# Attention and non-local block: one subtraction of the maxima a block, the weighted sum kept in the result's tile, and the halves of one sum of exponentials added ahead of the ones

## The chip, the cores and the metric

The kernel runs on one core of one Trainium2 chip. The metric is the device time of one execution in microseconds (us), as the median of several runs. TensorE (PE in the profile) does the matmuls, VectorE (DVE), ScalarE (ACT) and GpSimd (POOL) the rest of the arithmetic; SyncE (SP) issues DMAs, and GpSimd issues the DMAs that add while they copy.

## The reference

The input x has 2 images of 256 channels and 64 x 64 = 4096 places. Two layers follow each other. Only the first, an attention with 8 heads of 32 channels, is touched by most of the change:

```python
qkv = jnp.einsum('oc,bchw->bohw', w_qkv, x)
q, k, v = jnp.split(qkv, 3, axis=1)            # each to (b, 8, 32, 4096)
scores = jnp.einsum('bhdi,bhdj->bhij', q, k) / jnp.sqrt(32)
attn = jax.nn.softmax(scores, axis=-1)
out = jnp.einsum('bhij,bhdj->bhdi', attn, v)
x = jnp.einsum('oc,bchw->bohw', w_proj, out) + x
```

The second layer is a non-local block: two 1 x 1 convolutions and a third, two of them pooled 2 x 2, a softmax over 1024 pooled places, a weighted sum, a last convolution, a batch normalisation and the addition of x.

## The kernel before, in words

**Blocks and steps.** Four heads make a quad, so there are 2 images x 2 quads, numbered n = 0 to 3. The 4096 queries of a quad are cut into 8 blocks of 512 (i), so the attention has 32 blocks. A block goes over its 4096 keys in 32 steps of 128 (j). In a step (lines 534 to 569), for each of two pairs of heads, TensorE makes scores of 128 keys x 512 queries for two heads (`score`, L415) and ScalarE takes their exponential (L551). Then TensorE makes the weighted sum of the values of the step before for all four heads (`weigh`, L439), and VectorE adds it to the block's sum `num` (L450). In step 0 ScalarE copies instead of adding (L448).

**Scores by differences.** A pair of heads keeps one PSUM tile over several steps. At every fourth step (j % 4 == 0) the tile is begun anew: `subtract` (L427) writes minus the maximum of each query, as a product of ones with three bf16 terms of the maximum, and the scores of 128 keys are added to it. In the three steps after it, not the next keys are multiplied but the difference between the next keys and those before, so that the tile then holds the next scores. The keys of a quad (`k[n]`) lie in 8 chunks of 512, and four steps take the same 128 columns of four neighbouring chunks: chunk 1 - 0 lies in `kd[n]`, 2 - 1 in `mid_kd`, 3 - 2 in `kd[n]`, and for the upper four chunks in `last_kd`, `mid_kd`, `last_kd`. GpSimd makes these differences: L219 and L241 in the prologue, and at each change of quad L234 (twice 1024 columns) and L241.

**Maxima.** `maxima` finds the maximum of every query, a little over one block ahead of the exponentials: further products (L264), of which VectorE reduces plain ones (L276), while for half of heads 2 and 3's chunks ScalarE takes the positive part of a product with a difference (L283) and VectorE reduces the sum (L290). Each `advance(maxes)` issues two such products. They use `k`, `kd` and `last_kd`, but in block 0 of a later quad not `last_kd`. `negate` then makes the three terms on GpSimd (L141 to L145), and `make_rows` turns them with TensorE (L150).

**Sums of the exponentials.** A step has two tiles of exponentials: a single one of heads 0 and 1 (six buffers) and half of a double one of heads 2 and 3 (five buffers). `add` collects them: GpSimd adds the singles to the block's first single (L469) except that of step 31, which stays apart; the doubles are added by DMAs that add (L477), in turn to two partial sums. `normalize`, for the block before, is a generator that the steps of the next block advance at j = 2 and from j = 6 on (AFTER). At j = 2 it merges the two partial sums by one more such DMA (L483). At j = 6 TensorE multiplies what is left with ones (L495): for heads 0 and 1 the sum and step 31's exponentials, for heads 2 and 3 the two halves of the merged double, two rounds over four heads. ScalarE copies the denominators (L503), SyncE brings them into a form in which VectorE inverts few elements (L512 to L521), and some 18 steps later GpSimd multiplies `num` by them and writes the result's tile `y` (L526). The blocks that end a batch don't merge and have four rounds.

**What sets the order.** Each engine works off its own queue in order. The framework forms the queues from the program's order and the tiles' dependencies and adds the waits; `tc.issue_after(x)` puts an instruction behind x on x's engine. Beside the attention, `make` projects one piece of q, k or v of what comes next after steps 11, 19 and 27 (L186, L198).

**Second layer.** `non_local` keeps its running sums of exponentials in the tile `sum1`, of the same two buffers as `num` (L706).

Of the kernel before, what the change touches and what calls it, by code (L numbers as in the profile page):

```python
# [9 lines left out]
F32 = mybir.dt.float32  # L10
# [6 lines left out]
N = HH * WW  # L17
# [5 lines left out]
P = 128  # L23
# [12 lines left out]
def conv_attention(  # L36
# [131 lines left out]
    def make(what, n, i):  # L168
        b, qd = QUAD[n]
        if (b, i) not in held:  # L170
            name = f"x_{what}_{n}_{i}"
            if attending:
                held.clear()
                to = xs.tile([P, NC, NB], F32, tag="x", name=name)
            else:
                to = single(name)
            held[b, i] = load_x(b, i, to)
        xc = held[b, i]
        name = f"{what}_{b}_{qd}_{i}"
        pq = scratch(name)  # L180
        if what == "v":
            if i == 0:
                v[n] = qkv.tile([P, NJ, QH, D], F32, tag="v", name=f"v_{n}")
            for j in range(NB // P):
                for c in range(NC):
                    nc.tensor.matmul(  # L186
                        pq[:, bass.ts(j, P)],
                        xc[:, c, bass.ts(j, P)],
                        wv_sb[:, c, bass.ts(qd, P)],
                        start=(c == 0),  # L190
                        stop=(c == NC - 1),
                    )
                if j % 2 == 1:
                    yield
            nc.scalar.copy(v[n][:, bass.ts(i, NB // P)].rearrange("p j h d -> p (j h d)"), pq)
            return
        for c in range(NC):
            nc.tensor.matmul(  # L198
                pq,
                wqk_sb[:, c, qd, 0 if what == "q" else 1, :],  # L200
                xc[:, c, :],
                start=(c == 0),
                stop=(c == NC - 1),
            )
            yield
        if what == "q":
            to = q[n, i] = qkv.tile([P, NB], F32, tag="q", name=f"q_{n}_{i}", bufs=3)
        else:
            if i == 0:
                k[n] = qkv.tile([P, N], F32, tag="k", name=f"k_{n}")  # L210
            to = k[n][:, bass.ts(i, NB)]
        nc.scalar.copy(to, pq)
        if what == "k" and i % 4 == 2 and n == 0:
            between(n, i // 4)
        if what == "k" and i % 2 == 1 and n == 0:
            if i == 1:
                kd[n] = qkv.tile([P, NI // 4, NB], F32, tag="kd", name=f"kd_{n}")
            two = k[n][:, bass.ts(i // 2, 2 * NB)]
            nc.gpsimd.tensor_sub(  # L219
                (kd[n] if i < NI // 2 else last_kd)[:, i // 2 % (NI // 4), :],  # L220
                two[:, NB:],
                two[:, :NB],
            )
        elif what == "k" and i == NI // 2 - 1:
            kd[n] = qkv.tile([P, NI // 4, NB], F32, tag="kd", name=f"kd_{n}")
            differences(n, 0, kd[n])

    last_kd = const.tile([P, NI // 4, NB], F32, name="last_kd")  # L230

    def differences(n, half, to):
        two = k[n][:, bass.ts(half, N // 2)].rearrange("p (c t n) -> p c t n", t=2, n=NB)
        nc.gpsimd.tensor_sub(to, two[:, :, 1, :], two[:, :, 0, :])  # L234


    mid_kd = const.tile([P, 2, NB], F32, name="mid_kd")

    def between(n, half):
        two = k[n][:, N // 2 * half + NB :]  # L240
        nc.gpsimd.tensor_sub(mid_kd[:, half, :], two[:, NB : 2 * NB], two[:, :NB])  # L241

# [143 lines left out]
    def attend(b, y):  # L388
        class Block:


            def __init__(self, qd, i):
                self.n, self.qd, self.i = QUAD.index((b, qd)), qd, i
                self.name = f"{b}_{qd}_{i}"
                self.rows = self.n * NI + i
                self.num = None
                self.sums = {}
                self.last = []

        def keys(j):  # L400

            return j // 16 * 16 + j % 4 * 4 + j % 16 // 4

        def score(s, pair, blk, j):

            half, c, cols = j // 16, j % 4, bass.ts(j % 16 // 4, P)
            if c == 0:
                kj = k[blk.n][:, bass.ts(keys(j), P)]
            elif c == 2:
                kj = mid_kd[:, half, cols]  # L410
            else:
                kj = (last_kd if half else kd[blk.n])[:, c // 2, cols]
            for t in range(2):
                h = 2 * pair + t
                nc.tensor.matmul(  # L415
                    s[:, t, :],
                    kj[bass.ts(h, D), :],
                    q[blk.n, blk.i][bass.ts(h, D), :],
                    start=False,
                    stop=True,  # L420
                    skip_group_check=j % 4 > 0,
                )

        def subtract(s, pair, blk):
# [10 lines left out]
        def weigh(blk, j, p):  # L435

            w = scratch(f"w_{blk.name}_{j}")
            for h in range(QH):
                nc.tensor.matmul(  # L439
                    w[bass.ts(h, D), :],  # L440
                    v[blk.n][:, keys(j), h, :],
                    p[h // 2][:, h % 2, :],
                    start=True,
                    stop=True,
                )
            if j == 0:
                blk.num = work.tile([P, NB], F32, tag="num", name=f"num_{blk.name}")
                nc.scalar.copy(blk.num, w)  # L448
            else:
                nc.vector.tensor_add(blk.num, blk.num, w)  # L450

        DIRECT = 1
        added = None

        def add(blk, j, p, two):
            nonlocal added
            if j == 0:  # L460
                blk.sums[0] = p[0]
            elif j % 2 and (blk.n, blk.i) == (len(QUAD) - 1, NI - 1):

                if j == 1:
                    blk.last.append(p[0])
                else:
                    nc.vector.tensor_add(blk.last[0], blk.last[0], p[0])
            elif j < NJ - DIRECT:
                added = nc.gpsimd.tensor_add(blk.sums[0], blk.sums[0], p[0])  # L469
            else:  # L470
                blk.last.append(p[0])
            if j % 2:
                n = 1 + j // 2 % 2
                if j < 4:
                    blk.sums[n] = two
                else:
                    nc.gpsimd.dma_start(out=blk.sums[n], in_=two, accum_op=ALU.add)  # L477

        def normalize(blk):
            whole = [1, 2]  # L480
            if (blk.qd, blk.i) != (QUADS - 1, NI - 1):
                with tc.issue_after(added.ins):
                    nc.gpsimd.dma_start(out=blk.sums[1], in_=blk.sums[2], accum_op=ALU.add)  # L483
                whole = [1]
                yield
            den = scratch(f"den_{blk.name}")
            mine = [
                [blk.sums[0], *blk.last],
                [blk.sums[n][:, j] for j in range(2) for n in whole],
            ]  # L490
            for n in range(max(map(len, mine))):
                for h in range(QH):
                    those = mine[h // 2]
# [29 lines left out]
                for _ in range(13):  # L523
                    yield
            with tc.issue_after(added.ins):
                nc.gpsimd.tensor_mul(y[:, blk.qd, bass.ts(blk.i, NB)], blk.num, r)  # L526

        waiting, normal = None, iter(())
        for qd in range(QUADS):
            for i in range(NI):  # L530
# [3 lines left out]
                for j in range(NJ):  # L534
# [1 line left out]
                        two = double(f"p_{blk.name}_{j}_1")  # L536
                    p = [single(f"p_{blk.name}_{j}_0"), two[:, j % 2]]
                    for pair in (1, 0):
                        if j % 4 == 0:
                            s = both[pair] = scores(f"s_{blk.name}_{j}_{pair}")  # L540
                            subtract(s, pair, blk)
                            advance(maxes)
# [12 lines left out]
                            normal = normalize(waiting[0])  # L555
                    add(blk, j, p, two)
                    waiting = blk, j, p
                    if j == 2 or j >= AFTER:
                        advance(normal)
                    if j % 2 == 0:  # L560
                        make_rows()
                        if (i, j) == (0, 2) and blk.n > 0:
                            between(blk.n, 1)
                        if (i, j) == (0, NJ // 4) and blk.n > 0:
                            differences(blk.n, 1, last_kd)
                        if (i, j) == (NI - 1, NJ // 2 + 2) and blk.n + 1 < len(QUAD):
                            between(blk.n + 1, 0)
                    elif j % 8 == 3 and j > 8 and items:
                        advance(make(*items.pop(0)), 9)
        weigh(*waiting)  # L570
# [26 lines left out]

    def non_local(b, y, theta_w, phi_w):
        theta = [double(f"theta_{b}_{t}") for t in range(2)]
        theta = [t[:, a, c, :] for t in theta for a in range(2) for c in range(2)]  # L600

        kv = qkv.tile([P, M + NC * M + M - 2 * P], F32, tag="k", name=f"kv_{b}")
# [100 lines left out]
        def weigh(i, t, p):  # L703
            if t == 0:
                acc[i] = [scratch(f"y_{b}_{i}_0"), scratch(f"y_{b}_{i}_1")]
                acc[i].append(work.tile([P, NB], F32, tag="num", name=f"sum1_{b}_{i}"))  # L706
                nc.gpsimd.tensor_add(acc[i][NC], p[:, 0, :], p[:, 1, :])
            else:

# [65 lines left out]


    LEAD = 4
    AFTER = 6
    attending = False


# [77 lines left out]
```

## Time and profile before

| What | Value |
| --- | --- |
| Median of 3 runs | 3987.23 us (3986.58 to 3989.69) |
| Profiled execution, its own time | 3986.4 us |
| Its span, first to last instruction | 3984.6 us |
| Busy of the span: PE, DVE, POOL, ACT | 99%, 74%, 73%, 67% |
| Mean share of the DMA engines in an attention block | 0.80 (1253 to 1357 us) |
| An attention block with maxima | about 104 us |
| Granted clock of TensorE | 0.997 |

A line of the groups has the line of code, engine, operation, output and inputs, their shapes and the count, then the busy time in us and the mean of one in ns, then the idle time of the engine just before, and what ended it. A line of the timeline has the start and the duration in us; neighbours of one kind are merged (x8 is eight instructions), and brackets hold the idle time before. PE stands for matmuls, PEld for loads of weights. An f32 matmul appears as two instructions. Shapes such as 32*128 are rows x columns of the array that a matmul uses.

### The profile page before, as it was taken

To read this page: it belongs to the slowest core of one execution; us is meant where nothing else is said; L and a number is where in the kernel's file an instruction comes from. 1 tells how busy PE (TensorE), PEld (TensorE's weight loads), DVE (VectorE), ACT (ScalarE), POOL (GpSimd) and SP (SyncE) were. 2 spreads that over 40 slices of the span, in tenths; PEclk is the share of its full clock that TensorE was granted. 3 is DMA by queue.
4 is the path that set the end of the run, shared out by engine and by line. 5 is a ranking of instruction groups with operands and counts; after the bars stand their busy time and mean duration, and the time that the engine had idled before them with its cause. 6 is when DMAs were issued, how large, how long until landed. Compare 5 with 4: busy or idle time off the path is not lost.

```text
span 3984.6 us, 72269 instructions
## 1 busy us (share of the span) xinstructions
PE 3949.7 (99%) x28592; PEld 1450.9 (36%) x28592; DVE 2937.8 (74%) x5451; ACT 2671.5 (67%) x3328; POOL 2903.6 (73%) x1851
## 2 busy tenths in 40 slices
PE   8999999999999999999999999999999999999998
PEld 4333333333333333333333333333333333333333
DVE  5877877788777787774457877787888888884434
ACT  4777777777777777751137777777677777777121
POOL 1888888888888888871448888888888888886043
PEclk9999999999999999999999999999999999999999
DMA  1777877887777777880017788878787778778200
GB/s 56 146 160 165 166 165 164 170 166 163 165 162 164 163 165 164 170 198 8 22 39 163 165 166 166 173 165 170 162 173 164 164 165 166 163 163 182 66 16 27
DMA packets 113941, 569.56 MB, mean 143 GB/s; under 512 B 20296, under 2 KB 22600, under 8 KB 52416
## 3 DMA queue, kind: packets, MB, share of 16 engines
q0 software_dynamic: 68832, 501.25, 62.8%
q1 hardware_dynamic: 44080, 62.88, 4.5%
q8 instruction: 224, 3.67, 0.4%
q14 instruction: 117, 0.96, 0.1%
q10 hardware_dynamic: 688, 0.79, 0.1%
HBM read 54.78 MB, written 8.88 MB: 16 GB/s over the span
## 4 chain that ended last, share of the span: by engine, by line
PE 97%; DVE 2%; DMA 0%; ACT 0%; POOL 0%; issue 0%; DVEq 0%; ACTq 0%
PE w L439 26%; PE ps L264 26%; PE s L415 24%; PE y L715 6%; PE s L427 3%; PE q L198 2%; PE v L186 2%; PE k L198 2%; PE den L495 1%; PE g L640 1%; DVE r L729 1%; PE f L683 1%; PE proj L584 1%; PE f L749 1%; PE tp L624 0%; PE tp L620 0%
## 5 line engine op out<-in xcount | busy, mean ns | idle before, releaser
L469 POOL TENSOR_TENSOR p<-p,p 128x1024 f32<-128x1024 f32 x945 | 2324.7, 2460 | 557.0 <-ACT p L551 550.1
L551 ACT ACTIVATE p<-s 128x1024 f32<-128x1024 f32 x2048 | 2089.9, 1025 | 624.1 <-PE ps L264 408.5
L264 PE MATMUL ps<-k,q 32*128 32x512 f32 x6232 | 2049.0, 627 | 4.0 <-DVE part L276 1.7
L276 DVE TENSOR_REDUCE part<-ps 128x1 f32<-128x512 f32 x2136 | 1369.9, 686 | 574.2 <-PE ps L264 557.7
L439 PE MATMUL w<-p,v 128*32 128x512 f32 x8192 | 1091.0, 605 | 0.7 <-ACT p L551 0.7
L450 DVE TENSOR_TENSOR num<-num,w 128x512 f32<-128x512 f32 x992 | 681.4, 687 | 92.7 <-PE w L439 91.3
L290 DVE CUSTOM_DVE_ANT_0 ps<-ps,over 128x512 f32<-128x512 f32 x980 | 676.0, 693 | 32.1 <-PE ps L264 27.9
L264 PEld LDWEIGHTS ps<-k,q 32*128 32x128 f32 x6232 | 636.5, 183 | 55.7 <-DVE num L450 8.7
L283 ACT ACTIVATE over<-ps 128x512 f32<-128x512 f32 x916 | 543.2, 593 | 15.2 <-PE ps L264 14.0
L264 PE MATMUL ps<-kd,q 32*128 32x512 f32 x1056 | 518.2, 595 | 0.7 <-POOL kd L219 0.7
L415 PE MATMUL s<-q,k 32*128 32x512 f32 x2048 | 513.2, 590 | 0.0
L415 PE MATMUL s<-q,kd 32*128 32x512 f32 x2048 | 511.1, 616 | 0.4 <-ACT p L551 0.3
L415 PE MATMUL s<-q,mid_kd 32*128 32x512 f32 x2048 | 510.1, 614 | 0.0
L415 PE MATMUL s<-q,last_kd 32*128 32x512 f32 x2048 | 506.8, 614 | 0.0
L439 PEld LDWEIGHTS w<-p,v 128*32 128x32 f32 x8192 | 161.1, 108 | 799.0 <-DVE part L276 769.4
L264 PE MATMUL ps<-last_kd,q 32*128 32x512 f32 x904 | 437.4, 590 | 1.5 <-POOL last_kd L219 1.5
L477 POOL DMA_DIRECT2D p<-p x448 | 395.5, 883 | 33.4 <-ACT p L551 28.7
L415 PEld LDWEIGHTS s<-q,mid_kd 32*128 32x128 f32 x2048 | 173.0, 183 | 309.7 <-ACT over L283 197.1
L415 PEld LDWEIGHTS s<-q,kd 32*128 32x128 f32 x2048 | 174.6, 184 | 282.2 <-ACT over L283 177.8
L415 PEld LDWEIGHTS s<-q,last_kd 32*128 32x128 f32 x2048 | 173.1, 183 | 269.6 <-ACT over L283 164.3
L715 PE MATMUL y<-p,kv 128*128 128x512 f32 x512 | 240.0, 608 | 6.4 <-DVE r L729 6.4
L764 ACT ACTIVATE p<-f 128x1024 f32<-128x1024 f32 x64 | 65.6, 1025 | 248.4 <-PE f L749 219.1
(108 smaller groups left out, 2720.4 us busy)
## 6 DMA issues: line engine op xcount, KB each, us to landing
p<-p POOLq DMA_DIRECT2D x478, 1024.0 KB, 7.5
x_k<-in_x_dram SPq DMA_DIRECT2D x32, 512.0 KB
x_q<-in_x_dram SPq DMA_DIRECT2D x30, 512.0 KB
x_res<-in_x_dram SPq DMA_DIRECT2D x16, 512.0 KB
out_dram<-z SPq DMA_DIRECT2D x16, 512.0 KB
r<-flat SPq DMA_DIRECT2D x120, 64.0 KB
x_v<-in_x_dram SPq DMA_DIRECT2D x6, 512.0 KB
wqk_sb<-in_wqk_dram ACTq DMA_DIRECT2D x1, 512.0 KB
```

Of the source, the lines that this page charges most:

```text
L198: nc.tensor.matmul(pq, wqk_sb[:, c, qd, 0 if what == "q" else 1, :], xc[:, c, :], start=(c == 0), stop=(c == NC - 1),)
L264: nc.tensor.matmul(ps, q[n, i][bass.ts(h, D), bass.ts(g, P)], keys[bass.ts(h, D), :], start=True, stop=True,)
L276: reduced = nc.vector.tensor_reduce(part[:, g, h, j : j + 1], ps, AX.X, ALU.max)
L283: cut = nc.scalar.activation(over, ps, AF.Relu)
L290: reduced = nc.vector.tensor_tensor_reduce(out=ps, in0=ps, in1=over, scale=1.0, scalar=LEAST, op0=ALU.add, op1=ALU.max, accum_out=part[:, ...
L415: nc.tensor.matmul(s[:, t, :], kj[bass.ts(h, D), :], q[blk.n, blk.i][bass.ts(h, D), :], start=False, stop=True, skip_group_check=j % 4 > 0,)
L439: nc.tensor.matmul(w[bass.ts(h, D), :], v[blk.n][:, keys(j), h, :], p[h // 2][:, h % 2, :], start=True, stop=True,)
L450: nc.vector.tensor_add(blk.num, blk.num, w)
L469: added = nc.gpsimd.tensor_add(blk.sums[0], blk.sums[0], p[0])
L477: nc.gpsimd.dma_start(out=blk.sums[n], in_=two, accum_op=ALU.add)
L551: nc.scalar.activation(p[pair], s, AF.Exp, scale=scale)
L715: nc.tensor.matmul(acc[i][o], wg[:, 2 * t + j, bass.ts(o, P)], p[:, j, :], **edge)
```

## The change

1. Only step 0 of a block begins its two PSUM tiles and subtracts the maxima. All later steps multiply by differences. The order of keys becomes the same 128 columns of all 8 chunks, then the next 128. Three more kinds of differences are needed: between chunks 4 and 3 (`mid_kd` has three now), and, for the turn from the last chunk to the next columns of the first, `turn_kd`.
2. GpSimd makes the differences in pieces of 512 columns or fewer, at other places: in the prologue as the keys appear, at a change of quad in steps 26, 28 and 30 of the last block and in steps 0 and 2 of the next.
3. The block's weighted sum lies in its place in `y` from the start. VectorE, not ScalarE, copies it at step 0, and GpSimd multiplies it there.
4. GpSimd adds step 31's single, behind the last accumulating DMA. For heads 2 and 3 the merge is put at j = 1, and at j = 5 GpSimd adds the two halves of the merged double into a single tile; the ones at j = 8 (AFTER) then take one round.
5. The running sums of the second layer lie in a double tile, four in turn instead of two.

```diff
 # make(), after a piece of q or k is copied
-        if what == "k" and i % 4 == 2 and n == 0:
-            between(n, i // 4)
+        if what == "k" and i % 2 == 0 and i > 0 and n == 0:
+            between(n, i // 2 - 1)
+        if what == "k" and i == NI - 1 and n == 0:
+            rounds(n)
         if what == "k" and i % 2 == 1 and n == 0:
...
+            differences(n, i // 2, (kd[n] if i < NI // 2 else last_kd)[:, i // 2 % (NI // 4), :])
         elif what == "k" and i == NI // 2 - 1:
             kd[n] = qkv.tile([P, NI // 4, NB], F32, tag="kd", name=f"kd_{n}")
-            differences(n, 0, kd[n])
+            for c in range(2):
+                differences(n, c, kd[n][:, c, :])
...
+    def differences(n, c, to):
+        two = k[n][:, bass.ts(c, 2 * NB)]
+        nc.gpsimd.tensor_sub(to, two[:, NB:], two[:, :NB])
...
+    mid_kd = const.tile([P, NI // 2 - 1, NB], F32, name="mid_kd")
+    turn_kd = const.tile([P, NB // P - 1, P], F32, name="turn_kd")
+
+    def between(n, c):
+        two = k[n][:, NB * (2 * c + 1) : NB * (2 * c + 3)]
+        nc.gpsimd.tensor_sub(mid_kd[:, c, :], two[:, NB:], two[:, :NB])
+
+    def rounds(n):
+        nc.gpsimd.tensor_sub(
+            turn_kd,
+            k[n][:, P:NB].rearrange("p (a n) -> p a n", n=P),
+            k[n][:, N - NB : N - P].rearrange("p (a n) -> p a n", n=P),
+        )
+
+    def renew(i, j, n):
+        if (i, j) == (NI - 1, NJ - 6):
+            between(n + 1, 0)
+        elif (i, j) == (NI - 1, NJ - 4):
+            between(n + 1, 1)
+        elif (i, j) == (NI - 1, NJ - 2):
+            differences(n + 1, 2, last_kd[:, 0, :])
+            between(n + 1, 2)
+        elif (i, j) == (0, 0):
+            differences(n, 3, last_kd[:, 1, :])
+        elif (i, j) == (0, 2):
+            rounds(n)
...
-                self.num = None
+                self.num = y[:, qd, bass.ts(i, NB)]
...
         def keys(j):
-            return j // 16 * 16 + j % 4 * 4 + j % 16 // 4
+            return j % NI * (NB // P) + j // NI

         def score(s, pair, blk, j):
-            half, c, cols = j // 16, j % 4, bass.ts(j % 16 // 4, P)
...
+            c, a = j % NI, j // NI
+            if j == 0:
+                kj = k[blk.n][:, :P]
+            elif c == 0:
+                kj = turn_kd[:, a - 1, :]
             else:
-                kj = (last_kd if half else kd[blk.n])[:, c // 2, cols]
+                made = mid_kd if c % 2 == 0 else kd[blk.n] if c < NI // 2 else last_kd
+                at = c // 2 - 1 if c % 2 == 0 else c // 2 % 2
+                kj = made[:, at, bass.ts(a, P)]
...
             if j == 0:
-                blk.num = work.tile([P, NB], F32, tag="num", name=f"num_{blk.name}")
-                nc.scalar.copy(blk.num, w)
+                nc.vector.tensor_copy(blk.num, w)
...
-            elif j < NJ - DIRECT:
+            elif j < NJ - 1:
                 added = nc.gpsimd.tensor_add(blk.sums[0], blk.sums[0], p[0])
-            else:
-                blk.last.append(p[0])
...
-                    nc.gpsimd.dma_start(out=blk.sums[n], in_=two, accum_op=ALU.add)
+                    sent = nc.gpsimd.dma_start(out=blk.sums[n], in_=two, accum_op=ALU.add)
+            if j == NJ - 1 and (blk.n, blk.i) != (len(QUAD) - 1, NI - 1):
+                with tc.issue_after(sent.ins):
+                    added = nc.gpsimd.tensor_add(blk.sums[0], blk.sums[0], p[0])

         def normalize(blk):
-            whole = [1, 2]
+            theirs = [blk.sums[n][:, j] for j in range(2) for n in (1, 2)]
             if (blk.qd, blk.i) != (QUADS - 1, NI - 1):
                 with tc.issue_after(added.ins):
                     nc.gpsimd.dma_start(out=blk.sums[1], in_=blk.sums[2], accum_op=ALU.add)
-                whole = [1]
+                yield
+                theirs = [single(f"whole_{blk.name}")]
+                with tc.issue_after(added.ins):
+                    nc.gpsimd.tensor_add(theirs[0], blk.sums[1][:, 0], blk.sums[1][:, 1])
                 yield
...
-                nc.gpsimd.tensor_mul(y[:, blk.qd, bass.ts(blk.i, NB)], blk.num, r)
+                nc.gpsimd.tensor_mul(blk.num, blk.num, r)
...
-                        if j % 4 == 0:
+                        if j == 0:
                             s = both[pair] = scores(f"s_{blk.name}_{j}_{pair}")
                             subtract(s, pair, blk)
...
-                    if j == 2 or j >= AFTER:
+                    if j in (1, 5) or j >= AFTER:
                         advance(normal)
                     if j % 2 == 0:
                         make_rows()
...
+                        if i > 0 and blk.n + 1 < len(QUAD) or i == 0 and blk.n > 0:
+                            with tc.issue_after(added.ins) if added else ExitStack():
+                                renew(i, j, blk.n)
...
+        sums = double(f"sums1_{b}")
...
-                acc[i].append(work.tile([P, NB], F32, tag="num", name=f"sum1_{b}_{i}"))
+                acc[i].append(sums[:, i // 2 % 2, i % 2, :])
...
-    AFTER = 6
+    AFTER = 8
```

More of the change, by code (lines that the diff above doesn't have):

```diff
@@ L217, in make @@
                 kd[n] = qkv.tile([P, NI // 4, NB], F32, tag="kd", name=f"kd_{n}")
[L218 to L223, printed above, removed]
+            differences(n, i // 2, (kd[n] if i < NI // 2 else last_kd)[:, i // 2 % (NI // 4), :])
         elif what == "k" and i == NI // 2 - 1:
             kd[n] = qkv.tile([P, NI // 4, NB], F32, tag="kd", name=f"kd_{n}")
-            differences(n, 0, kd[n])
+            for c in range(2):
+                differences(n, c, kd[n][:, c, :])
     last_kd = const.tile([P, NI // 4, NB], F32, name="last_kd")
[L232 to L241, printed above, removed]
+    def differences(n, c, to):
[24 more added lines that the diff above has]
+            rounds(n)
     def during(n, i):
@@ L400, in keys @@
         def keys(j):
-            return j // 16 * 16 + j % 4 * 4 + j % 16 // 4
+            return j % NI * (NB // P) + j // NI
         def score(s, pair, blk, j):
-            half, c, cols = j // 16, j % 4, bass.ts(j % 16 // 4, P)
[L407 to L410, printed above, removed]
-            else:
-                kj = (last_kd if half else kd[blk.n])[:, c // 2, cols]
+            c, a = j % NI, j // NI
[3 more added lines that the diff above has]
+                kj = turn_kd[:, a - 1, :]
+            else:
+                made = mid_kd if c % 2 == 0 else kd[blk.n] if c < NI // 2 else last_kd
+                at = c // 2 - 1 if c % 2 == 0 else c // 2 % 2
+                kj = made[:, at, bass.ts(a, P)]
             for t in range(2):
@@ L420, in score @@
                     stop=True,
-                    skip_group_check=j % 4 > 0,
+                    skip_group_check=j > 0,
                 )
@@ L446, in weigh @@
             if j == 0:
-                blk.num = work.tile([P, NB], F32, tag="num", name=f"num_{blk.name}")
-                nc.scalar.copy(blk.num, w)
+                nc.vector.tensor_copy(blk.num, w)
             else:
                 nc.vector.tensor_add(blk.num, blk.num, w)
-        DIRECT = 1
         added = None
@@ L483, in normalize @@
                     nc.gpsimd.dma_start(out=blk.sums[1], in_=blk.sums[2], accum_op=ALU.add)
-                whole = [1]
+                yield
+                theirs = [single(f"whole_{blk.name}")]
+                with tc.issue_after(added.ins):
+                    nc.gpsimd.tensor_add(theirs[0], blk.sums[1][:, 0], blk.sums[1][:, 1])
                 yield
             den = scratch(f"den_{blk.name}")
[L487 to L490, printed above, removed]
+            mine = [[blk.sums[0], *blk.last], theirs]
             for n in range(max(map(len, mine))):
@@ L561, in attend @@
                         make_rows()
[L562 to L567, printed above, removed]
+                        if i > 0 and blk.n + 1 < len(QUAD) or i == 0 and blk.n > 0:
+                            with tc.issue_after(added.ins) if added else ExitStack():
+                                renew(i, j, blk.n)
                     elif j % 8 == 3 and j > 8 and items:
```

## The prediction

> **What bounds the kernel now.** I read the engines' busy times and the chain that ended last first, then the groups of instructions, then the timeline of TensorE alone and of GpSimd alone over two blocks, then the waits.
>
> ```profile
> PE 3949.7 (99%) x28592; PEld 1450.9 (36%) x28592; DVE 2937.8 (74%) x5451; ACT 2671.5 (67%) x3328; POOL 2903.6 (73%) x1851
> ...
> PE 97%; DVE 2%; DMA 0%; ACT 0%; POOL 0%; issue 0%; DVEq 0%; ACTq 0%
> ```
>
> TensorE (PE) is busy nearly all the time and makes up 97% of the chain. Its ends are modelled, so I do not take durations from its busy time: a matmul of two heads stands beside matmuls of the other two. What counts is how much later the next step begins. The groups that the change touches:
>
> ```profile
> L469 POOL TENSOR_TENSOR p<-p,p 128x1024 f32<-128x1024 f32 x945 | 2324.7, 2460 | 557.0 <-ACT p L551 550.1 <-DMA p<-p 2.0 <-issue 0.2
> ...
> L427 PE MATMUL s<-rows,ones_b 32*128 32x512 bf16 x1024 | 199.4, 380 | 0.0
> ...
> L495 PE MATMUL den<-p,ones 128*32 128x512 f32 x528 | 65.1, 593 | 0.0
> ...
> L448 ACT COPY num<-w 128x512 f32<-128x512 f32 x32 | 19.1, 597 | 0.0
> ```
>
> Every step j of a block has one group of weigh matmuls (L439), so their starts are the clock of the steps:
>
> ```profile
> 1148.41 1.06 PE L439 MATMUL w<-p,v 128*32 128x512 f32 x8
> ...
> 1151.64 1.06 PE L439 MATMUL w<-p,v 128*32 128x512 f32 x8
> ...
> 1154.63 1.06 PE L439 MATMUL w<-p,v 128*32 128x512 f32 x8
> 1155.63 0.39 PE L427 MATMUL s<-rows,ones_b 32*128 32x512 bf16 x2
> ...
> 1157.77 1.06 PE L439 MATMUL w<-p,v 128*32 128x512 f32 x8
> ...
> 1160.72 1.06 PE L439 MATMUL w<-p,v 128*32 128x512 f32 x8
> ...
> 1163.68 1.06 PE L439 MATMUL w<-p,v 128*32 128x512 f32 x8
> 1164.57 1.90 PE L495 MATMUL den<-p,ones 128*32 128x512 f32 x16
> ...
> 1168.36 1.06 PE L439 MATMUL w<-p,v 128*32 128x512 f32 x8
> ```
>
> A plain step takes 2.96 us (1157.77 to 1160.72 to 1163.68). The step with the subtraction of the maxima takes 3.14 (1154.63 to 1157.77), the one with the denominators 4.68 (1163.68 to 1168.36), and the one in which ScalarE copies the first weighted sum 3.23 (1148.41 to 1151.64), the one after it 2.99. These four numbers carry the forecast. GpSimd at the same block boundary:
>
> ```profile
> 1143.11 0.87 POOL L477 DMA_DIRECT2D p<-p  x1
> 1150.14 2.36 POOL L469 TENSOR_TENSOR p<-p,p 128x1024 f32<-128x1024 f32 x1 [6.16 <-ACT p L551]
> 1153.15 2.37 POOL L469 TENSOR_TENSOR p<-p,p 128x1024 f32<-128x1024 f32 x1 [0.65 <-ACT p L551]
> 1155.46 0.86 POOL L483 DMA_DIRECT2D p<-p  x1
> ```
>
> It stands idle for 6.16 us at the boundary, where steps 31 and 0 have no addition. In a pair of plain steps (two additions, one DMA issue, 5.92 us) it has only about 0.4 us free. The waits of ScalarE show that buffers of exponentials are not short today:
>
> ```profile
> ACT p L551 <- DMA p<-p: 6.9, 5, 2.8
> ...
> ACT p L551 <- POOL p L469: 0.3, 1, 0.3
> ```
>
> [...] the group L427 is 199 us busy, and 1024 instructions in 256 steps, at 0.18 us more a step, add only some 46 us. [...] the merge of the two partial sums (L483) has to wait on GpSimd for the last accumulations of its block. No wait shows in front of it today.
>
> **The change part by part**, 32 blocks of 32 steps.
>
> 1. Subtractions. Seven of eight per block go (steps 4, 8, ... 28). Each costs 3.134 - 2.959 = 0.175 us (the medians over all blocks of the distances shown). In the three blocks that end a pair of batch and quad (the eighth, sixteenth, twenty-fourth), steps from about 12 to 27 take 3.1 to 3.3 us on VectorE, which then reduces four plain products per step; there four of the seven are hidden. In the last block, without maxima, I count none. So 31 x 7 - 12 = 205 times 0.175 = **35.9 us**. The new order of the former subtraction steps (scores, then maxima) is that of plain steps, so I price them at 2.96.
>
> 2. Denominators. Two rounds of ones on heads 0 to 3 (16 instructions, 1.72 us) become one (8), since the halves of heads 2 and 3 are added on GpSimd and step 31's exponentials go into the running sum. Half of 1.72 is 0.86, in 30 blocks: **25.8 us**. The two blocks that end a batch keep four rounds.
>
> 3. The copy at step 0. ScalarE's busy time in that step is 2 x 1.025 + 0.593 + 0.597 = 3.24 us, which is the step's 3.23: it is the limit there. VectorE takes the copy in the slot where it adds in any other step (0.687 us; it has 0.39 us idle in a plain step). The trace has no such VectorE copy. Below, nothing at all; above, the 0.687 us of the addition, which plain steps hide. I take the step at 2.96, so 0.27 + 0.03 = 0.30 us, 31 times: **9.3 us**.
>
> 4. GpSimd's extra work. Per block one addition for step 31 and one of the halves, 2 x 2.37 = 4.7 us on 88.2 busy in a block of 104 (a window of 1253 to 1357 us shows 88.17). The block falls to about 102, so GpSimd goes from 85% to 91%. Step 31's addition falls into the 6.16 us of idle time: cost 0. The halves at step 5 make the queue some 2 us late. Queued behind them are the additions of steps 6 and 7 and the DMA issue of step 7; ScalarE waits for those through the six buffers of single exponentials. Three of them are taken there (old sum, own sum, the halves' sum), so step j's exponential needs step j-3's addition finished: 3 x 2.96 - 1.03 - 2.37 = 5.5 us of room. A delay of 2 us costs TensorE nothing; without that cover it would be up to 2.37 us in 30 blocks, 71 us. It is worked off by the 0.4 us per two steps and by the projection at step 11, whose step takes 5.05 us. The denominators move from step 6 to step 8; the halves are ready about 3 us before. The multiplication of the result moves from about step 25 to 27, next to the casts of the maxima: 3 us late, again within the room.
>
> 5. The merge moves from behind the addition of step 2 to behind that of step 1, and now waits there, with step 2's addition queued behind it. The last accumulation is issued at 1143.11 and lands 7.5 us later (median), 1150.6; the addition of step 1 ends at 1152.5. So the wait is 0 at the median, and at the longest landing in the trace (12.9) 3.5 us, within the room. Its earlier landing releases a buffer that five exponentials waited for: a gain of at most 6.9 us, not counted.
>
> 6. New differences. At each of three changes of quad, GpSimd gets six subtractions of about 1.4 us or less (L241 has 1412 ns) in place of two and one of 2.8: about 2 us more. All but two now stand in steps 26 to 30 with the casts and multiplication, where by my count the queue gets 5 to 6 us late. TensorE needs each difference several steps later, but a buffer may be 1 or 2 us late: **3 us** over the kernel (0 to 15). In the prologue one subtraction stands ahead of the last difference that TensorE waits for: **1 us**.
>
> Sum: 35.9 + 25.8 + 9.3 - 3 - 1 = 67 us. The profiled execution took 3986.4 us (span 3984.6 and 1.8 around it): 3986.4 - 67 = 3919.4. The median of the runs is 0.9 higher, so I forecast **3920 us**.
>
> **The rivals.**
>
> a. GpSimd becomes late enough to be felt: its queue carries delays over the block, and TensorE waits at the denominators or through exponential buffers about 1 us a block. 3920 + 30 = 3950. For it: 91% busy, 0.4 us of slack a pair. Against it: 5.5 us of room, and 6 us of idle time at each boundary.
>
> b. The subtraction's time is not to be had, because the plain steps live on the slack that the long steps give: only parts 2 and 3 remain, 3987 - 35 + 4 = 3956. Against it: plain steps stay at 2.96 for three in a row after a long one, without growing.
>
> c. The chain is right: it gives the subtractions 2.7% of the span, 108 us, of which 7/8 are 94 in place of 36: 3920 - 58 = 3862. Against it: the step distances, which measure it directly.
>
> d. Slower. The weighted sum now lies in the result's tile, and if the order is kept by whole tile and not by region, each VectorE addition after the multiplication of the block before (one tile, two writers) waits for GpSimd's late queue: 3 us a block, 31 x 3 = 93 against 67 won, about 4013. It decides from 67/31 = 2.2 us a block. Against it: today one half of the middle differences is written while the other is still read, and no matmul waits for that write.
>
> **How the numbers follow.** Forecast 0.70, with 3906 to 3934 as its own range (part 6 at 15, part 5's 6.9, a tenth of the subtraction either way); a 0.12; b 0.09; c 0.04; d 0.05. The range 3904 to 3956 takes in the forecast and most of a and b, and leaves out c and d. About 0.2% (8 us) is what a measurement can tell from no change. Faster: the forecast, b, c and most of a, 0.91; the same 0.04, from a's worse end; slower 0.05.
>
> **What would show it.** Right: weigh starts 2.96 us apart at steps 4, 8, ... 28 as elsewhere; 128 matmuls in L427's group; 3.8 us for the step with the denominators; 2.96 for that after step 0; no new wait of ScalarE on GpSimd. Wrong: exponentials that wait for GpSimd or DMA in most blocks, denominators behind GpSimd, VectorE additions released by the multiplication, or plain steps over 2.96.

## The result and the profile after

| | before | after |
| --- | --- | --- |
| Median, us | 3987.04 (4 runs, 3986.58 to 3989.69) | 3922.90 (4 runs, 3920.21 to 3923.55) |
| Ratio, 95% interval | 1 | 0.9836 (0.9821 to 0.9851) |
| Profiled execution: its time, its span, us | 3986.4, 3984.6 | 3922.51, 3920.7 |
| POOL busy in a window over one block (104 and 102 us) | 88.17 us | 91.48 us |
| TensorE's granted clock | 0.997 | 0.997 |

The kernel is 64.1 us faster, a saving of 1.64%. The page of the kernel after has TensorE still busy nearly throughout:

```profile
PE 3882.0 (99%) x27452; PEld 1370.0 (35%) x27452; DVE 2940.4 (75%) x5483; ACT 2654.9 (68%) x3296; POOL 3051.9 (78%) x1926
...
PE 53%; DVE 2%; DMA 1%; ACT 0%; issue 0%; POOL 0%; DVEq 0%; ACTq 0%; POOLq 0%
```

The shares of the chain add up to 56% only: it could not be followed back to the start this time, and I read nothing from it. The groups of the kernel after that answer to the four of before, the ones with their two inputs apart:

```profile
L491 POOL TENSOR_TENSOR p<-p,p 128x1024 f32<-128x1024 f32 x945 | 2350.5, 2487 | 363.4 <-ACT p L574 338.4 <-PE w L463 16.0 <-DMA p<-p 0.4
...
L518 PE MATMUL den<-p,ones 128*32 128x512 f32 x164 | 38.1, 593 | 0.0
L518 PE MATMUL den<-whole,ones 128*32 128x512 f32 x120 | 30.9, 593 | 0.0
L451 PE MATMUL s<-rows,ones_b 32*128 32x512 bf16 x128 | 26.5, 386 | 0.0
...
L471 DVE COPY y<-w 128x512 f32<-128x512 f32 x32 | 22.1, 691 | 3.2 <-PE w L463 3.0
```

The subtractions fell from 1024 to 128, the matmuls with ones from 528 to 284. New beside them are 30 additions of halves (L510, 2.58 us each) and 31 of step 31's exponentials (L500). TensorE's timeline over the start of the twelfth block, its weigh matmuls and one of the two subtractions:

```profile
1224.86 1.07 PE L463 MATMUL w<-p,v 128*32 128x512 f32 x8
1225.86 0.39 PE L451 MATMUL s<-rows,ones_b 32*128 32x512 bf16 x2
...
1227.99 1.07 PE L463 MATMUL w<-p,v 128*32 128x512 f32 x8
...
1236.87 1.06 PE L463 MATMUL w<-p,v 128*32 128x512 f32 x8
1239.83 1.06 PE L463 MATMUL w<-p,v 128*32 128x512 f32 x8
...
1251.66 1.07 PE L463 MATMUL w<-p,v 128*32 128x512 f32 x8
...
1255.48 1.06 PE L463 MATMUL w<-p,v 128*32 128x512 f32 x8
```

Of the steps that had a subtraction, only step 0 still has the long distance (1224.86 to 1227.99, 3.13). The plain distance is 2.96 (1236.87 to 1239.83), now also where subtractions stood, and the distance with the denominators 3.82 (1251.66 to 1255.48). Block by block in both traces, weigh start to weigh start, the fifteen or so full blocks that nothing else disturbs went from 104.25 to 101.86 us each: 2.39 less, where seven subtractions at 0.175, half the denominators at 0.86 and the copy at 0.30 had promised 2.385. The whole ledger: the blocks, with the stretch between the two batches, won 68.3 us, the prologue lost 2.9 (first weigh at 103.10, now 105.98), and the stretch behind the last block lost 1.5, together 63.9 of span.

GpSimd at the same place of the same block:

```profile
1226.66 2.36 POOL L500 TENSOR_TENSOR p<-p,p 128x1024 f32<-128x1024 f32 x1
1232.67 2.37 POOL L491 TENSOR_TENSOR p<-p,p 128x1024 f32<-128x1024 f32 x1 [3.65 <-ACT p L574]
1234.98 0.86 POOL L506 DMA_DIRECT2D p<-p  x1
...
1246.90 2.58 POOL L510 TENSOR_TENSOR whole<-p 128x1024 f32<-128x1024 f32 x1
...
1268.05 2.36 POOL L491 TENSOR_TENSOR p<-p,p 128x1024 f32<-128x1024 f32 x1 [1.78 <-ACT p L574]
```

The addition of step 31 (L500) lies in what was idle time; 3.65 of the 6.16 us are left. The merge (L506) is issued without a wait. After the halves (L510) no bracket appears until 1268.05: GpSimd runs late and has caught up at the projection, some 19 us later. TensorE doesn't feel it. Of the waits of ScalarE and GpSimd that could show a late GpSimd, the kernel after has:

```profile
POOL p L506 <- DMA p<-p: 8.8, 4, 4.4
...
ACT p L574 <- POOL whole L510: 3.0, 2, 2.3
...
PEld den L518 <- POOL p L491: 12.6, 25, 0.5
```

The columns are the total in us, the number of waits and the longest. With two exponentials that waited for a DMA (2.7 us) and one for an addition (1.1) ScalarE has five such waits, 6.8 us in all, in place of six of 7.2 before; but two of them are of a kind that the prediction didn't name, on the halves (`whole`). The last line is also new: in 25 cases the loads of the ones' weights (PEld) wait up to 0.5 us for an addition of GpSimd. The step with the denominators is no longer for it, since 3.82 is what its half round was reckoned at.

### The profile page after: what moved, and what is told of

The parts are those of the page before. It is cut to its first block, busy times and chain, and to the rows that moved or that the text cites. A ratio compares the mean times of both kernels' runs of the same rounds, so it can differ in the third digit from the quotient of the medians.

```text
span 3920.7 us, 69957 instructions
## 1 busy us (share of the span) xinstructions
PE 3882.0 (99%) x27452; PEld 1370.0 (35%) x27452; DVE 2940.4 (75%) x5483; ACT 2654.9 (68%) x3296; POOL 3051.9 (78%) x1926
## 4 chain that ended last, share of the span: by engine, by line
PE 53%; DVE 2%; DMA 1%; ACT 0%; issue 0%; POOL 0%; DVEq 0%; ACTq 0%; POOLq 0%
PE s L439 14%; PE w L463 13%; PE ps L286 11%; PE y L736 6%; PE g L661 1%; DVE r L750 1%; PE f L704 1%; PE proj L604 1%; PE f L770 1%; PE q L198 1%; PE den L518 1%; PE tp L645 0%; PE tp L641 0%; PE v L186 0%; PE k L198 0%; DMA x_res<-in_x_dram 0%
## 5 line engine op out<-in xcount | busy, mean ns | idle before, releaser
L491 POOL TENSOR_TENSOR p<-p,p 128x1024 f32<-128x1024 f32 x945 | 2350.5, 2487 | 363.4 <-ACT p L574 338.4
L286 PE MATMUL ps<-k,q 32*128 32x512 f32 x6232 | 2016.1, 627 | 4.0 <-DVE part L298 1.7
L439 PE MATMUL s<-q,mid_kd 32*128 32x512 f32 x3072 | 767.4, 615 | 0.0
L473 DVE TENSOR_TENSOR y<-y,w 128x512 f32<-128x512 f32 x992 | 679.1, 685 | 47.1 <-PE w L463 46.4
L286 PEld LDWEIGHTS ps<-k,q 32*128 32x128 f32 x6232 | 628.1, 183 | 43.3 <-DVE part L298 8.9
L439 PEld LDWEIGHTS s<-q,mid_kd 32*128 32x128 f32 x3072 | 262.0, 183 | 413.9 <-ACT over L305 225.6
L785 ACT ACTIVATE p<-f 128x1024 f32<-128x1024 f32 x64 | 65.5, 1024 | 248.5 <-PE f L770 219.2
L732 POOL TENSOR_TENSOR sums<-sums,p 128x512 f32<-128x512 f32 x96 | 121.3, 1264 | 113.7 <-ACT p L785 109.9
```

The costliest lines, as they stand in the source:

```text
L286: nc.tensor.matmul(ps, q[n, i][bass.ts(h, D), bass.ts(g, P)], keys[bass.ts(h, D), :], start=True, stop=True,)
L439: nc.tensor.matmul(s[:, t, :], kj[bass.ts(h, D), :], q[blk.n, blk.i][bass.ts(h, D), :], start=False, stop=True, skip_group_check=j > 0,)
L732: nc.gpsimd.tensor_add(acc[i][NC], acc[i][NC], p[:, j, :])
```

## The experiments

The theory: each part gives what it frees on TensorE (or, at step 0, on ScalarE), and GpSimd's extra work is hidden. The rivals to tell apart: that the win has another source, and that GpSimd's cover is thinner than was reckoned. Times are compared with the kernel before on the same chip (3986.96 to 3987.97), and with the kernel after as its own runs gave it.

### The subtractions alone put back

```diff
-            if j == 0:
-                kj = k[blk.n][:, :P]
-            elif c == 0:
-                kj = turn_kd[:, a - 1, :]
+            if c % 4 == 0:
+                kj = k[blk.n][:, bass.ts(keys(j), P)]
...
-                        if j == 0:
+                        if j % 4 == 0:
                             s = both[pair] = scores(f"s_{blk.name}_{j}_{pair}")
```

> The changed kernel, with the seven subtractions per block put back (the pair's PSUM tile is begun anew at every fourth step, from plain keys); everything else as changed. My theory: each costs TensorE 0.175 us where no other engine limits the step, 205 of them, so 35.9 us over the changed kernel: about 3959. The rival that the chain's share is what they cost: 94 us, about 4017. The rival that plain steps live on slack from the long ones, so that nothing is lost when they come back: about 3923.

Measured: 3953.89 us (3951.84 to 3954.59), 0.9914 of before (0.9899 to 0.9929), 31.0 over the kernel after. Weigh matmuls (L461 here) in its TensorE timeline, with a subtraction between the first and the second:

```profile
1145.56 1.07 PE L461 MATMUL w<-p,v 128*32 128x512 f32 x8
...
1148.70 1.06 PE L461 MATMUL w<-p,v 128*32 128x512 f32 x8
...
1151.65 1.06 PE L461 MATMUL w<-p,v 128*32 128x512 f32 x8
```

3.14 us with a subtraction, 2.95 without: the price of 0.175 is right. Block by block, the undisturbed ones are 1.23 us longer than in the kernel after, which is 7 x 0.175. In the three blocks in which VectorE reduces four plain products a step it is 0.27 to 0.34 where three subtractions were counted (0.53), in the last seven full blocks mostly 1.06 where 1.23 were counted, and in the last block 0.45 where none was. All blocks together: 32.4 us. So the forecast's 205 subtractions were some 20 too many, and rivals b (0) and c (94 us) are out.

### The denominators alone as before

Two rounds at step 6, no halves, step 31's exponentials apart:

```diff
-                yield
-                theirs = [single(f"whole_{blk.name}")]
-                with tc.issue_after(added.ins):
-                    nc.gpsimd.tensor_add(theirs[0], blk.sums[1][:, 0], blk.sums[1][:, 1])
+                theirs = [blk.sums[1][:, j] for j in range(2)]
...
-                    if j in (1, 5) or j >= AFTER:
+                    if j == 2 or j >= AFTER:
...
-    AFTER = 8
+    AFTER = 6
```

> The changed kernel, with the denominators as before: two rounds of ones at step 6, step 31's exponentials multiplied by ones instead of added, no addition of halves on GpSimd. My theory: 0.86 us in 30 blocks comes back, 25.8 us, less the 1 to 2 us lost at the changes of quad to GpSimd's queue: 3947 to 3949. The rival that GpSimd's two more additions a block are felt by TensorE: about 1 us a block less, so 3919.

Measured: 3948.05 us (3947.17 to 3950.38), 0.9901 (0.9887 to 0.9916), 25.2 over the kernel after. An undisturbed block takes 0.856 us longer. All blocks together give 23.6 us in place of 25.8: the seventeenth, which had met low clock in the kernel after (0.50 from 2030.75 to 2037.57 us, with its first weigh at 2034.70), and the twenty-fifth, in which GpSimd was late there, are 1.36 and 0.57 us shorter here. The term of 0.86 a block stands, and the GpSimd work that comes with it costs nothing in such a block: taking it away gave nothing back.

### The copy at step 0 alone on ScalarE

```diff
-                nc.vector.tensor_copy(blk.num, w)
+                nc.scalar.copy(blk.num, w)
```

> The changed kernel, with ScalarE in place of VectorE copying the first weighted sum (still to the result's place). My theory: the step after is ScalarE's again, 0.27 and 0.03 us in 31 blocks, 9.3 us: about 3932. The rival that the 0.3 us went with another part of the change (ahead of it in the same step stood the merge at step 2): about 3923.

Measured: 3929.08 us (3927.39 to 3929.66), 0.9852 (0.9838 to 0.9867), 6.2 over the kernel after. In its trace ScalarE runs four exponentials, the copy (0.59 us) and two more instructions in a row with no idle time, from 1130.26 to 1135.64: it is the limit there. An undisturbed block takes 0.27 us longer. The 0.03 us that the forecast added for the next step doesn't come back, and over the blocks the sum is 7.8 us in place of 9.3. The difference to 6.2 lies mostly in the prologue (0.6 earlier) and behind the last block (0.6), neither of which the edit touches.

### The last difference ahead of the turn in the prologue

In the prologue GpSimd made `turn_kd` (1.00 us at 68.81) ahead of the last piece of `last_kd`, for which TensorE waits. The two calls change places:

```diff
-        if what == "k" and i == NI - 1 and n == 0:
-            rounds(n)
         if what == "k" and i % 2 == 1 and n == 0:
...
             differences(n, i // 2, (kd[n] if i < NI // 2 else last_kd)[:, i // 2 % (NI // 4), :])
+        if what == "k" and i == NI - 1 and n == 0:
+            rounds(n)
```

> The changed kernel, with the differences for the turn made after the last ordinary difference in the prologue and not before it. Theory one, from the trace (granted clock 0.58 from 71 to 74 us, after TensorE waited 1.69 us there): the longer wait also costs clock, so the first weigh matmul comes 2.8 us earlier: about 3920. Theory two: only the 0.95 us of the GpSimd instruction count: 1 us earlier: about 3922.

Measured: 3920.65 us (3917.27 to 3921.68), 0.9833 (0.9816 to 0.9849), 2.3 under the kernel after. TensorE in the kernel after, and the granted clock (the third column from the end of a window's line, which gives the stretch, its length and the busy time of PE, PEld, DVE, ACT and POOL):

```profile
71.08 1.73 PE L286 MATMUL ps<-last_kd,q 32*128 32x512 f32 x8 [1.69 <-POOL last_kd L232]
...
71.00:74.00 3.00, 2.92 (x14) 1.58 (x15) 0.38 (x2) 1.20 (x3) 0.02 (x1) 0.58 0.02 5
```

The same in this experiment:

```profile
69.58 1.14 PE L286 MATMUL ps<-last_kd,q 32*128 32x512 f32 x8 [0.74 <-POOL last_kd L232]
...
71.00:74.00 3.00, 3.00 (x28) 2.00 (x26) 0.99 (x3) 2.29 (x5) 0.00 (x0) 1.00 0.00 0
```

The wait is 0.95 us shorter, and eight matmuls that took 1.73 us behind the longer wait take 1.14: in the kernel after the wait ended at 71.08, and from 71.50 to 74.91 us, for 3.41 us, the granted clock was 0.50. From the end of this wait to that of the next long one TensorE needs 19.40 us there (71.08 to 90.48) and 17.85 here (69.58 to 87.43), so the low clock cost 1.55 us on top of the 0.95. That the longer wait costs clock too is as the first expectation has it, though the first weigh comes 2.06 us sooner than in the kernel after (103.92 against 105.98) and not 2.8. Seven of the traces here have the wait of 1.7 us. Six of them show the drop; the one with the copy on ScalarE shows none, and needs 17.84.

The next long wait is in all ten traces, that of the kernel before included: 1.69 us for VectorE's maxima. Half clock follows it too. First the kernel before, then this experiment:

```profile
87.70 1.13 PE L264 MATMUL ps<-k,q 32*128 32x512 f32 x4 [1.69 <-DVE part L276]
...
88.72:98.96 10.24, 10.20 (x36) 4.99 (x36) 6.17 (x13) 2.38 (x4) 0.00 (x0) 0.50 0.01 2
```

```profile
87.43 0.88 PE L286 MATMUL ps<-k,q 32*128 32x512 f32 x2 [1.69 <-DVE part L298]
...
87.81:101.46 13.65, 13.61 (x51) 7.39 (x51) 8.11 (x17) 3.58 (x6) 0.35 (x2) 0.50 0.00 1
```

The low clock lasts 10.24 us before and 13.65 here, and from the end of the wait to the first weigh it takes 15.40 us before and 16.49 here. So the first weigh comes 0.82 us later than in the kernel before (103.10), though the wait ended 0.27 earlier; that difference goes with the longer stretch at half clock. The kernel with ScalarE's copy has the long stretch too (16.48), the other traces have the short one (15.39 to 15.51), also the last experiment below, which has this experiment's order. So the stretch isn't the order's doing; why it is longer in two traces is open.

### The halves added twice, and three times

How far is GpSimd from being felt? The same addition is repeated, which leaves the values as they are and adds 2.4 us of GpSimd work a block at the tightest place, or 4.8.

```diff
-                    nc.gpsimd.tensor_add(theirs[0], blk.sums[1][:, 0], blk.sums[1][:, 1])
+                    for _ in range(2):
+                        nc.gpsimd.tensor_add(theirs[0], blk.sums[1][:, 0], blk.sums[1][:, 1])
```

> The changed kernel, with GpSimd's addition of the halves made twice in a row in each of 30 blocks (same result), 2.4 us more at step 5. My theory of room: in a steady block the halves are ready about 3.3 us before the denominators of step 8 start, and the exponentials have 5.5 us, so 2.4 us more are still covered: 3923 to 3930. The rival that GpSimd is already at its edge: each 2.4 us is felt, 30 times, so about 3994.

> The changed kernel, with the addition of the halves made three times, 4.8 us more at step 5. My theory of room: the denominators now start 1.5 to 2 us late in each of 30 blocks, so 3968 to 3983: still a little under the kernel before, and the cover is seen to end between the second and the third addition. The rival that only GpSimd's total counts (91.5 + 4.8 of a block of 102): still hidden, 3923 to 3930.

Measured: 3942.11 us for two (3941.15 to 3943.41; 0.9887, 0.9870 to 0.9903), and 4017.26 for three (4015.22 to 4019.06; 1.0076, 1.0061 to 1.0091), which is slower than the kernel before. An undisturbed block takes 0.51 and 2.94 us longer. So the first 2.4 us are nearly hidden, and the next 2.4 are felt in full: the room is about 2.4 - 0.5 = 1.9 us. The forecast had 5.5, and my expectations for both runs, made with a larger room, are too low. ScalarE's waits for the halves with two additions:

```profile
ACT p L575 <- POOL whole L511: 51.4, 29, 4.6
```

and those of ScalarE and of the denominators' loads with three:

```profile
ACT p L575 <- POOL whole L511: 125.9, 30, 7.1
PEld den L519 <- POOL whole L511: 70.5, 57, 4.8
```

ScalarE's exponentials wait for the halves 29 and 30 times, once a block, not for the buffers of single exponentials that the forecast had in mind, but for the double one that the halves' addition reads and then frees. The denominators wait too, for 16.8 us in all with two additions. Which of the two costs the time is not decided by these lines.

### Three times, and the denominators two steps later

```diff
-    AFTER = 8
+    AFTER = 10
```

> The halves are added three times, as in the run before it (4017.3 us), and the denominators stand two steps later, at step 10 in place of step 8 (the division and the multiplication behind them move by two steps too). Theory 1: the first to wait for the late halves is the exponential of step 8 of heads 2 and 3, which needs the double buffer that the halves' addition frees. It waits as before, so the time stays at 4017 within about 8 us (some 2.9 us a block over the changed kernel), while the wait of the denominators for the halves goes. Theory 2: the denominators, which stood at step 8, are the ones that cost the time. Two steps are 5.9 us, more than the 4.9 us added, so the loss goes and the time falls to the changed kernel's 3923, or to 3942, the time with one extra addition, at most.

Measured: 4064.76 us (4059.68 to 4065.97), 1.0190 of before (1.0173 to 1.0207): neither of the two expectations. The denominators' wait is gone from the list, and the other is as it was:

```profile
ACT p L575 <- POOL whole L511: 128.1, 30, 6.9
```

So the second theory falls: what costs the time there is the exponential of heads 2 and 3 in step 8. That it became 47.5 us worse is seen in the tenth block, where this exponential waits 4.29 us (4.04 in the run before). First TensorE's timeline there, then a window with the granted clock:

```profile
1095.94 1.22 PE L439 MATMUL s<-q,kd 32*128 32x512 f32 x2 [2.98 <-ACT p L575]
```

```profile
1096.00:1098.00 2.00, 2.00 (x11) 1.56 (x15) 0.00 (x0) 1.29 (x2) 2.00 (x3) 0.50 0.00 0
```

Two things were added. The denominators had lain partly within the stall; at step 10 they cost their 0.86 us beside it, and the stall is not shorter: 0.41 us a block net (the fourteenth block, at full clock, has 105.19 in place of 104.79). And TensorE, with nothing in the stall, idles 2.98 us in one piece and comes back at half clock (0.50 above). Of the 28 blocks with such a wait (2.64 to 3.50 us), 21 show the lower clock in the four microseconds behind it. At full clock the distance to the next weigh start is 6.26 us; over the 28 blocks it is 29.9 us longer than that in all, and the distance after it 6.5. These 36.4 and 28 x 0.41 = 11.5 make 48 us, where those blocks lost 45.

### The turn made ahead of the change of quad

The prologue's order as above, and at a change of quad `turn_kd` in the last block's step 24 in place of step 2 of the next, where it stands ahead of the halves:

```diff
+        elif (i, j) == (NI - 1, NJ - 8):
+            rounds(n + 1)
...
-        elif (i, j) == (0, 2):
-            rounds(n)
```

> The changed kernel with the prologue's order of the fourth experiment, and at a change of quad the differences for the turn made at step 24 of the block before (the last step that reads the old ones) instead of at step 2 of the new block. Theory: GpSimd is 1.3 us less late at step 8 after a change of quad, where an exponential waited 2.3 us for the halves in the block from 2856 us on; that wait goes, 1.2 to 1.7 us, and with the prologue's 2 us it makes about 3919. The rival: the landing of the last accumulating DMA sets that wait, not the queue behind it: no gain over the fourth experiment, 3920.6.

Measured: 3918.13 us (3917.74 to 3919.18), 0.9828 (0.9813 to 0.9843): 4.8 us under the kernel after and the fastest kernel here. Its lead over the prologue's order alone, 2.5 us, is no more than these runs can tell apart (3917.27 to 3921.68 there). In the trace the twenty-fifth block, the first of the last quad, is 0.80 us shorter than with the prologue's order alone. There GpSimd's queue had been latest, as its timeline in the kernel after shows:

```profile
2863.05 0.87 POOL L506 DMA_DIRECT2D p<-p  x1 [2.61 <-DMA p<-p]
...
2866.00 1.27 POOL L244 TENSOR_TENSOR turn_kd<-k 128x384 f32<-128x384 f32 x1
```

The merge waits 2.61 us for a DMA, the addition behind it in the queue starts only then (2863.66), the turn adds 1.27 us, and the halves end at 2877.5 (2874.91 + 2.62), late enough for the exponential of step 8 to wait 2.3 us, the longest of the waits for `whole` above.

## Why the prediction was right, point by point

The forecast was 3920 us, the median is 3922.9. Of the 67 us of the sum, 63.9 came (span against span); the blocks gave what was forecast for them (68.3 against 35.9 + 25.8 + 9.3 - 3 = 68.0), with errors that cancel, and the prologue and the end lost 3.4 us more. That the blocks' sum met so closely is luck: what the first three experiments give back over the blocks is 32.4, 23.6 and 7.8 us, 63.8 together, and the other 4.5 of the 68.3 are not assigned to a part. Most of them stand in three blocks, the seventeenth, the twenty-fifth and the last.

- **Part 1, subtractions.** Price right (0.175), count too high: 32.4 us in place of 35.9. In the blocks that VectorE limits three wins were counted and about two came. In the undisturbed blocks every step that lost its subtraction and holds no projection is at 2.96.
- **Part 2, denominators.** Right: 0.859 us less in the step that has them (4.675 to 3.816), 0.856 more when they alone are put back.
- **Part 3, the copy.** 0.27 a block in place of 0.30: ScalarE's part stands, the 0.03 of the next step isn't due to the copy. VectorE's copy takes 691 ns, as the addition that priced it, and is hidden like it.
- **Part 4, GpSimd's work.** That it is hidden is right, and so are the early work-off by step 11 and the halves ready 3 us before the denominators (1249.5 against 1252.5). The room of 5.5 us is wrong: about 1.9. It was reckoned from single buffers. The first to wait is the exponential of step 8 of heads 2 and 3: it started at 1250.93 in the block shown, 1.5 us after the halves' end. It needs a double buffer, and the halves' addition is what frees one. The same queue looked at through all its readers could have shown it.
- **Part 5, the merge.** Right at the median: 26 of 30 merges don't wait. Four do, 8.8 us in all. The longest, 4.4 in the last block, and the next, 2.6 at the change of quad above, are more than the room of 1.9.
- **Part 6, the differences.** At the changes of quad 1.7 us of the 3: the twenty-fifth block won 0.67 in place of 2.40, the ninth lost nothing. The seventeenth has 1.07 us more at its start, in a stretch of low clock (0.50 until 2037.57 us), which is in only one of the eight experiments, so I don't count it. The prologue lost 2.9 in place of 1: the 0.95 us of the wait are as forecast, the 1.55 of low clock behind it were not foreseen, and 0.28 were lost ahead of the first difference (TensorE's first wait for one ends at 33.91 before and 34.19 after), where the change does nothing. The 1.5 us behind the last block were not forecast either; that stretch differs by up to 4 us between kernels that share its code (292.8 to 297.0 us).

The rivals. **a** didn't happen: undisturbed blocks gained the full 2.40 us. It was nearer than its chance of 0.12 said: one addition more costs 19 us, two more 94. **b** and **c** are out by the first experiment (31 us, not 0 and not 94). **d** has no trace: VectorE's additions and the copy (L473, L471) wait for TensorE only (46.4 us in 64 waits, 3.0 in two), never for the multiplication (L549). A version with the sum in a tile of its own was not tried.

## What to carry to other kernels

The distance between starts of one recurring instruction on the bounding engine, with the edit's step against a plain one, gave prices that held to a hundredth of a microsecond for the subtractions and the denominators and to three hundredths for the copy; count separately the stretches in which another engine limits, since there a removed instruction gave less (0.27 to 0.34 us in place of 0.53 in the blocks that VectorE limits). Work put on GpSimd, which had slack, was hidden only up to the smallest room among all buffers that wait behind it (1.9 us, where the single buffers alone had given 5.5): list for each moved or added instruction every buffer that it frees, not only those of its own kind, and measure the room by doubling the work. Where a stall can't be avoided, leave independent work of the bounding engine in it: with the denominators moved out of the stall, the kernel with three additions took 47.5 us more.

## What the runs showed that I had not expected

A short idle time of TensorE cost nearly its length again in clock. After 1.7 us of idle in the prologue the granted clock was 0.50 for 3.41 us in six of seven kernels, which cost some 1.6 us, and after the second such wait for 10.24 or 13.65 us in all ten. After 2.6 to 3.5 us it was 0.50 in 21 of 28 blocks of the kernel with three additions and late denominators, where it made a step longer, mostly by 1.1 to 1.7 us; waits of 0.74 us (the prologue of the fourth experiment) and 0.83 us (a block with three additions) left it at 1.00.

What decides whether a wait brings the drop is not shown. Its length alone doesn't: waits of the same 2.7 us do and don't bring it. Stretches of low clock measured here lasted 3.41, 6.83 (2061.62 to 2068.45 us in the kernel before, behind a wait of 1.32), 10.24 and 13.65 us, that is one, two, three and four times 3.41. These lines of the kernel with three additions and late denominators, which begin whole multiples of 3.41 us apart, have stretches of that length (stretch, length, busy time of PE first, the clock third from the end), the first two of the tenth block, which had the drop, the other two of the nineteenth, which had none:

```profile
1092.58:1095.99 3.41, 0.43 (x7) 0.05 (x3) 1.14 (x3) 1.12 (x2) 3.41 (x2) 1.00 0.00 0
1095.99:1099.40 3.41, 3.41 (x16) 2.06 (x16) 1.29 (x2) 2.33 (x3) 3.41 (x3) 0.50 0.37 77
2338.44:2341.86 3.42, 1.65 (x16) 0.16 (x8) 2.41 (x5) 0.13 (x1) 3.34 (x3) 1.00 0.01 2
2341.86:2345.27 3.41, 2.46 (x16) 0.91 (x16) 1.25 (x2) 3.21 (x4) 3.41 (x3) 1.00 0.01 2
```

TensorE was busy for 0.43 us of the first stretch, and for 1.65 and 2.46 of the other two, over which its wait of 2.71 us is spread. In 19 of the 21 blocks with the drop it was busy for 13 to 45% of the 3.41 us ahead of the drop (54 and 59% in the other two); the drops in the prologue came after 3.41 us in which TensorE was busy for 50 or 51%, one after 65%. In the seven without it, divided in the same steps, it was busy for 46 to 51% of the emptiest stretch, and the kernel with ScalarE's copy kept its clock behind one that was 50% busy. So the share doesn't separate the cases sharply either.
